# First store of a pairwise product held for a later load piece, and its last three pairs sent in nine transfers of falling height

## The chip, the cores and the metric

The kernel runs on one core of one Trainium2 chip. The metric is device time in microseconds for one execution: the median of several runs, each without the profiler's own account. One further execution was profiled; its trace is what the views below are read from.

## The reference

For 4096 samples with 32 fields of 64 numbers each, every field is multiplied by a 64 x 64 matrix, and then every pair of fields (i < j, 496 pairs) gives the elementwise product of the raw field i and the transformed field j:

```python
vid = jnp.einsum('bfd,de->bfe', x, W)            # x: (4096, 32, 64), W: (64, 64), float32
idx_i, idx_j = jnp.triu_indices(F_, k=1)         # 496 pairs
return x[:, idx_i, :] * vid[:, idx_j, :]         # (4096, 496, 64)
```

The input is 33.6 MB, the output 520 MB, so nearly all the traffic is stores.

## The kernel before, in words

**Layout.** The 128 partitions hold two halves of the batch, 64 embedding numbers each. The free dimension counts in units of `C` = 128 samples, 512 bytes per partition: one unit is one field of a tile, or one pair of the output. The batch makes 16 tiles of 32 fields. Everything lives in one buffer `mem` of 445 units per partition; inputs and output slots are places in it, written out by hand in `XPLACE` (where each tile's fields go) and `SLOTS` (pairs in a slot, its first unit, and where the slot is cut because part of its space comes free earlier). A slot of 96 pairs is thus 128 rows of 49152 bytes, one row per partition.

**Work on one tile.** TensorE makes `vid` (all 32 transformed fields, in PSUM) with eight matmuls (line 172). VectorE then makes the 496 products tile by tile (line 196), in blocks that reuse one field against many, and writes them into the current slot. When the last pair of a slot is done, the slot is stored by one transfer (line 199). There are 70 slots over the 16 tiles; the slots run on across tile borders.

**Order of the work.** The order on SyncE (which issues every transfer) and on VectorE is the program's own. Slots share space: slot 0 (units 221 to 316) is overwritten by slot 2 (200 to 315), so VectorE waits for a store to land before it refills that space. SyncE issues in order, so a transfer that has to wait holds back every later one.

**Loads.** Tile 0 comes in two transfers (lines 136 and 140). The other tiles come in three groups. Right at the start, before the loop, tiles 1 to 3 are loaded in one transfer of 96 fields, and tiles 5 and 4 (64 fields) in two pieces given by `CUTS` (line 153): 38 fields and then 26. Two more groups of five tiles follow later, each in three pieces of which the last is 26 fields.

**The hold.** The first store after each group of loads is made to wait until the last piece but one has landed:

```python
store = nc.sync.dma_start(out=out[:, begin:end, :], in_=ot)
if pieces:
    behind(store, pieces[-2])
    pieces.clear()
```

`behind` adds a dependency: the later instruction is issued when the earlier transfer has landed. For the first store this means: when only the last 26 fields of the load are left.

**Completion semaphores.** Every transfer signals its landing on a semaphore. In the built program the transfers take them in turn from a set of eight (DMAHW0 to DMAHW7), and a transfer whose semaphore was used eight transfers earlier is issued after that one has landed, unless SyncE has waited for it already.

Of the kernel before, what the change touches and what calls it, by code (L numbers as in the profile page):

```python
# [21 lines left out]
    [[6, 7, 8, 9, 10]],  # L22
    [[15, 14, 13, 12, 11]],
]
CUTS = [[None, [(0, 38), (38, 64)]], [(0, 127), (127, 134), (134, 160)], [(33, 160), (26, 33), (0, 26)]]
XPLACE = [317, 349, 381, 413, 32, 0, 285, 317, 349, 381, 413, 128, 96, 64, 32, 0]


# [9 lines left out]
    (126, 247), (127, 96), (109, 223), (112, 333), (127, 158), (127, 285), (127, 64, 94),  # L38
    (127, 192, 93), (124, 320), (120, 48), (127, 190), (124, 317), (125, 158),
]  # L40


PAD = 24
# [9 lines left out]
def by_block():  # L53


    def within(lo):
        yield "step", lo, 2, 1, 0
        for k in range(2):
            yield "step", lo, 4, 2, k
        for i in (lo, lo + 8):  # L60
            yield "row", i + 4, i, 4, 4
        yield "row", lo + 8, lo, 8, 8

    yield from within(0)
    yield "row", 16, 0, 16, 16
    yield from within(16)


def products(blocks, at=0):

    for kind, a, b, c, d in blocks:
        if kind == "row":
            rows, n, i0, di, j0, dj = c, d, b, 0, a, 1
        else:
            rows, n, i0, di, j0, dj = 16 // b, c, a, b, a + c + d, b
        r = k = 0
        while r < rows:
            room = BREAKS[bisect_right(BREAKS, at)] - at
            if k or room < n:
                m, w = 1, min(n - k, room)  # L80
            else:
                m, w = min(rows - r, room // n), n
            yield at, m, w, i0 + r * di + k, di, j0 + r * dj, dj
            at += m * w
            if k + w == n:
                r, k = r + m, 0
            else:
                k += w
# [10 lines left out]
@with_exitstack  # L99
def pairwise_bilinear_kernel(  # L100
    ctx: ExitStack,
    tc: tile.TileContext,
    x0: bass.AP,
    x: bass.AP,
    out: bass.AP,
):

    nc = tc.nc
    NT = sum(len(tiles) for group in GROUPS for tiles in group)
    F = x0.shape[1] - 1 - PAD0
    D = P // 2
    NP = F * (F - 1) // 2

    BANK = 512 // C


    ctx.enter_context(tc.manual_schedule(engines={mybir.EngineType.SP, mybir.EngineType.DVE}))

    const = ctx.enter_context(tc.tile_pool(name="const", bufs=1))
    psum = ctx.enter_context(
        tc.tile_pool(name="ps", bufs=1, space=bass.MemoryType.PSUM)
    )
    vid = psum.tile([P, F, C], F32)

    mem = const.tile([P, UNITS, C], F32)


    w2 = const.tile([P, P], F32)


    place = XPLACE[0]
    nc.sync.dma_start(
        out=mem.rearrange("p u c -> p (u c)")[:, place * C - D : (place + F // 2) * C],
        in_=x0.rearrange("p u c -> p (u c)")[:, C - D : (1 + F // 2) * C],
    )
    nc.sync.dma_start(out=mem[:, place + F // 2 : place + F, :], in_=x0[:, 1 + F // 2 : 1 + F, :])  # L140
    nc.vector.memset(w2, 0.0)  # L141
    for half in (slice(0, D), slice(D, P)):
        nc.vector.tensor_copy(w2[half, half], mem[half, place - 1, C - D :])  # L143
    loaded = 1

    def load(tiles, cuts=()):
        nonlocal loaded
        n = len(tiles) * F
        place = XPLACE[tiles[0]]
        at = (loaded - 1) * F  # L150
        loaded += len(tiles)
        return [
            nc.sync.dma_start(out=mem[:, place + lo : place + hi, :], in_=x[:, at + lo : at + hi, :])  # L153
            for lo, hi in cuts or [(0, n)]
        ]

    ready = mybir.DependencyInfo(mybir.DependencyClass.Sync, mybir.DependencyReason.DATA)

    def behind(later, earlier):
        tc.add_manual_dep(later.ins, earlier.ins.name, ready, reason="issued when that has landed")  # L160

    pieces = []
    groups, cuts = iter(GROUPS), iter(CUTS)
    for tiles, parts in zip(next(groups)[1:], next(cuts)):
        pieces = load(tiles, parts)

    for t in range(NT):
        xt = mem[:, XPLACE[t] : XPLACE[t] + F, :]


        for b in range(0, F, BANK):
            nc.tensor.matmul(  # L172
                vid[:, b : b + BANK, :],
                lhsT=w2,
                rhs=xt[:, b : b + BANK, :],
                start=True,
                stop=True,
            )

        for at, m, w, i, di, j, dj in products(by_block(), t * NP):  # L180
            slot = bisect_right(STARTS, at) - 1
            n = m * w
            begin, end = STARTS[slot], STARTS[slot + 1]
            ot = mem[:, SLOTS[slot][1] : SLOTS[slot][1] + SLOTS[slot][0], :]
            o = ot[:, at - begin : at - begin + n, :]
            if m == 1:
                left = xt[:, i : i + w, :]
                right = vid[:, j : j + 1, :].to_broadcast([P, w, C])
            else:
                o = o.rearrange("p (m w) c -> p m w c", m=m)  # L190
                right = vid[:, j : j + (m - 1) * dj + 1 : dj, :].unsqueeze(2).to_broadcast([P, m, w, C])
                if di == 0:
                    left = xt[:, i : i + w, :].unsqueeze(1).to_broadcast([P, m, w, C])
                else:
                    left = xt.rearrange("p (m d) c -> p m d c", d=di)[:, i // di : i // di + m, i % di : i % di + w, :]
            nc.vector.tensor_tensor(o, left, right, ALU.mult)  # L196
            at += n
            if at == end:
                store = nc.sync.dma_start(out=out[:, begin:end, :], in_=ot)  # L199
                if pieces:  # L200
                    behind(store, pieces[-2])
                    pieces.clear()


        if t + 2 == loaded < NT:
            (tiles,) = next(groups)
            pieces = load(tiles, next(cuts))
# [45 lines left out]
```

## Time and profile before

| | |
|---|---|
| median of 3 runs | 1286.8 us (1286.73 to 1287.43) |
| the profiled execution's own time | 1287.24 us |
| its span, first to last instruction | 1285.5 us |
| VectorE busy | 1084.0 us, 84% |
| TensorE matmul busy | 231.1 us, 18% |
| DMA queue | 553.69 MB, 99.8% of 16 engines' span |
| first store issued; slot 1's; slot 2's | 28.78; 41.95; 61.49 us |

The busy share of an engine is time in instructions over the span. The share of the DMA queue is the time of its packets over 16 engines' span: 100% means that every one of the 16 engines always has a packet in hand. A packet is one row of a transfer (one partition's contiguous bytes), or the small write that signals an engine's part of a transfer as landed. SPq is SyncE's queue: the time shown beside a transfer there is that of issuing it, not of moving its bytes. The columns of a wait are: who waited (engine and line), for whom, us in total, times, longest us.

### The profile page before, as it was taken

Reading aid. Unit: us, or ns where it says so; the run is one execution under the profiler, and the core shown is the slowest. Engines: PE = TensorE matmul, PEld = TensorE weight load, DVE = VectorE, ACT = ScalarE, POOL = GpSimd, SP = SyncE. Lnnn points to the kernel's source line nnn. Section 1 sums busy time; section 2 is a strip of 40 time slices with the busy share of each in tenths; the row PEclk is TensorE's granted clock in tenths of the full one; section 3 lists DMA queues with packets and bytes.
Section 4 is the critical chain, followed back from the end, with each engine's and each line's share of the span. In section 5 each row is a group of like instructions: output and inputs, shape, how many; then the busy total and the mean of one; then the engine's idle time right before and its main releaser. Section 6 shows DMA issues by size and latency. Waiting matters only on the chain.

```text
span 1285.5 us, 1143 instructions
## 1 busy us (share of the span) xinstructions
PE 231.1 (18%) x256; PEld 67.7 (5%) x256; DVE 1084.0 (84%) x348; POOL 0.2 (0%) x4
## 2 busy tenths in 40 slices
PE   5031121303120212040311211103122130312000
PEld 1000000100000000010000000000000010000000
DVE  6889998899967389899799992849998889999952
POOL 0000000000000000000000000000000000000000
PEclk8555565556555556555565555556555555555555
DMA  9999999999999999999999999999999999999998
GB/s 400 438 429 438 436 428 438 431 435 436 432 430 439 416 433 425 445 430 433 439 427 441 435 429 436 419 432 429 440 432 440 429 430 441 429 441 430 434 436 370
DMA packets 11670, 553.75 MB, mean 431 GB/s; under 512 B 1296, under 2 KB 1296, under 8 KB 1552
## 3 DMA queue, kind: packets, MB, share of 16 engines
q1 hardware_dynamic: 11664, 553.69, 99.8%
q8 instruction: 2, 0.03, 0.0%
q14 instruction: 4, 0.03, 0.0%
HBM read 33.59 MB, written 520.09 MB: 431 GB/s over the span
## 4 chain that ended last, share of the span: by engine, by line
DVE 47%; DMA 44%; issue 6%; PE 0%; DVEq 0%; SPq 0%
DVE mem L196 47%; DMA out_dram<-mem 41%; DMA mem<-in_r_x_dram 3%; PE vid L172 0%; DVEq L241 0%; DVEq L196 0%; DVE w L143 0%; SPq L153 0%; DVEq L143 0%; SPq L199 0%
## 5 line engine op out<-in xcount | busy, mean ns | idle before, releaser
L196 DVE TENSOR_TENSOR mem<-mem,vid 128x1024 f32<-128x1024 f32 (+17 forms) x345 | 1083.4, 3212 | 170.5 <-DMA out_dram<-mem 164.2
L172 PE MATMUL vid<-mem,w 128*128 128x512 f32 x256 | 231.1, 1039 | 951.3 <-DVE mem L196 843.8
L172 PEld LDWEIGHTS vid<-mem,w 128*128 128x128 f32 x256 | 67.7, 306 | 1113.5 <-DVE mem L196 1011.9
L143 DVE COPY w<-mem 64x64 f32<-64x64 f32 x2 | 0.4, 190 | 5.0 <-DMA mem<-in_r_x_dram 4.9
L141 DVE MEMSET w<- 128x128 f32 x1 | 0.2, 165 | 0.8 <-PEq L221 0.8
L221 POOL MEMSET const-bfloat16-1.0<- 128x1 bf16 x1 | 0.1, 101 | 0.0
L221 POOL MEMSET const-uint8-127<- 128x1 uint8 x1 | 0.1, 101 | 0.0
L221 POOL MEMSET const-float32-0.0<- 128x1 f32 x1 | 0.1, 98 | 0.2 <-issue 0.2
L221 POOL MEMSET const-float32-1.0<- 128x1 f32 x1 | 0.1, 98 | 0.0
## 6 DMA issues: line engine op xcount, KB each, us to landing
out_dram<-mem SPq DMA_DIRECT2D x15, 8128.0 KB, 27.4
out_dram<-mem SPq DMA_DIRECT2D x14, 7680.0 KB, 24.9
out_dram<-mem SPq DMA_DIRECT2D x6, 7168.0 KB, 26.2
out_dram<-mem SPq DMA_DIRECT2D x5, 7936.0 KB, 28.2
out_dram<-mem SPq DMA_DIRECT2D x3, 7424.0 KB, 22.6
out_dram<-mem SPq DMA_DIRECT2D x3, 5888.0 KB, 20.9
mem<-in_r_x_dram SPq DMA_DIRECT2D x2, 8128.0 KB, 37.6
out_dram<-mem SPq DMA_DIRECT2D x2, 8064.0 KB, 24.3
```

The lines of the kernel that those rows point to most:

```text
L141: nc.vector.memset(w2, 0.0)
L143: nc.vector.tensor_copy(w2[half, half], mem[half, place - 1, C - D :])
L172: nc.tensor.matmul(vid[:, b : b + BANK, :], lhsT=w2, rhs=xt[:, b : b + BANK, :], start=True, stop=True,)
L196: nc.vector.tensor_tensor(o, left, right, ALU.mult)
L221: nc = _bacc.Bacc("TRN2", target_bir_lowering=False, num_devices=1, dynamic_dma_scratch_size=512)
```

## The change

Two things are edited. The cut of the second load piece moves from field 38 to field 51, so that the first store is issued when 13 fields of the load are left instead of 26. And slot 0's store sends only its first 93 pairs as one transfer; its last three pairs (`TAIL`) go out in nine transfers that take the partitions in turn: 64 of them, then 14, 12, 10, 8, 8, 6, 4 and 2 (`ROWS`), with 1536 bytes per partition each. All nine stand behind the 93-pair store and ahead of slot 1's store on SyncE. The dependency of the hold is on the 93-pair store. All other slots are stored as before.

```diff
-CUTS = [[None, [(0, 38), (38, 64)]], [(0, 127), (127, 134), (134, 160)], [(33, 160), (26, 33), (0, 26)]]
+CUTS = [[None, [(0, 51), (51, 64)]], [(0, 127), (127, 134), (134, 160)], [(33, 160), (26, 33), (0, 26)]]
...
+TAIL = 3
+ROWS = [64, 14, 12, 10, 8, 8, 6, 4, 2]
...
             if at == end:
-                store = nc.sync.dma_start(out=out[:, begin:end, :], in_=ot)
+                cut = SLOTS[slot][0] - (TAIL if slot == 0 else 0)
+                store = nc.sync.dma_start(out=out[:, begin : begin + cut, :], in_=ot[:, :cut, :])
+                if begin + cut < end:
+                    for lo, n in zip(accumulate([0, *ROWS]), ROWS):
+                        rows = slice(lo, lo + n)
+                        nc.sync.dma_start(out=out[rows, begin + cut : end, :], in_=ot[rows, cut:, :])
                 if pieces:
                     behind(store, pieces[-2])
                     pieces.clear()
```

## The prediction

> **What bounds the kernel now.** I read the page from its second part down: who is busy in every slice, the queue that carries it, then the first 80 us by engine, and last SyncE's own waits.
>
> ```profile
> span 1285.5 us, 1143 instructions
> ...
> PE 231.1 (18%) x256; PEld 67.7 (5%) x256; DVE 1084.0 (84%) x348; POOL 0.2 (0%) x4
> ...
> DMA  9999999999999999999999999999999999999998
> ...
> q1 hardware_dynamic: 11664, 553.69, 99.8%
> HBM read 33.59 MB, written 520.09 MB: 431 GB/s over the span
> ```
>
> The DMA row is nine in every slice but the last, and the one queue occupies 99.8% of 16 engines' span. VectorE is busy 84%. So the kernel is the time of 553.69 MB through 16 DMA engines, plus whatever idle or slowed time an engine picks up. The end is set by the engine that picked up most.
>
> The trace's packet records give that per engine. A store of 96 pairs is 128 rows of 49152 B, eight on each engine, and an undisturbed row takes 1.815 us; a 13312 B row (26 fields) takes 0.498, a 3584 B row 0.140. Following each engine's rows from transfer to transfer:
>
> ```
> end of transfer, us             first    mean     last engine
> load piece of 38 fields          27.51    27.88    28.30
> load piece of 26 fields          31.53    32.42    33.57
> store of slot 0                  46.03    46.91    48.07
> store before the second load    404.83   405.32   405.57
> last store                     1281.39  1282.04  1284.28
> ```
>
> Subtracting undisturbed row times leaves lateness. It grows where loads turn into stores: mean and worst engine go from 2.62 and 3.05 us to 3.20 and 4.35 at 33 us, from 4.15 and 4.55 to 4.65 and 6.45 at 430 us, and from 5.47 and 6.49 to 5.77 and 7.91 at 833 us. It ends at 6.12 and 8.35. Ahead of the second and third loads the early engines are slowed towards the latest one (mean 3.52 to 4.07 at 404 us, worst unchanged at 4.33). So **what counts is how late the last engine is**; an early engine's lead is not kept.
>
> SyncE around the first hold, from its waits between 28 and 64 us and its timeline to 70 us:
>
> ```profile
> SPq L199 <- DVE mem L196: 32.3, 3, 19.2
> SPq L199 <- DMA mem<-in_r_x_dram: 25.3, 1, 25.3
> ```
>
> ```profile
> 0.73 0.37 SPq L136 DMA_DIRECT2D mem<-in_r_x_dram  x1
> 1.16 0.42 SPq L140 DMA_DIRECT2D mem<-in_r_x_dram  x1
> 1.63 1.80 SPq L153 DMA_DIRECT2D mem<-in_r_x_dram  x3
> 28.78 33.04 SPq L199 DMA_DIRECT2D out_dram<-mem  x3
> ```
>
> The first store waits 25.3 us for the 38-field piece and then 0.3 for VectorE, and goes out at 28.78. The three stores of the last line begin at 28.78, 41.95 and 61.49: slot 1 is issued four us before the first engine finishes slot 0 (46.03), so no engine runs dry.
>
> [...] rows follow each other without a gap at the 46 us change. [...] this trace shows 1.0 (issue at 0.73, first row at 1.735)[...].
>
> **The change part by part.**
>
> *The hold.* 51 fields land instead of 38. A 26112 B row costs 0.724 + 6656 x 36.8 ps = 0.969 us (36.8 ps per byte is 1.675 us over 45568 B, from the rows above), eight rows take 1.96 us more, so the piece ends at 30.25 on the last engine instead of 28.30. VectorE finished at 28.78 and no longer matters; the store goes out at about 30.4, 1.65 us later. In before, rows of the last piece begin to stretch at 29.98, which is 1.2 us after the issue (0.498 grows to as much as 1.2 us), and cost 0.58 us in the mean and 1.30 on the worst engine. After: 30.4 + 1.2 = 31.6, when undisturbed loads end between 31.5 and 32.3. Most of that stretch goes: the last engine would end the loads at 32.3 to 32.8 instead of 33.57, **a gain of 0.8 to 1.3 us there**. It may instead leave a gap of up to 0.5 us on the first engines, whose lead counts for nothing. Nothing else is issued in that time on SyncE.
>
> *The split.* Slot 0's store becomes 93 pairs (rows of 47616 B, 1.759 us) and nine transfers of 1536 B rows, each an estimated 0.140 - 2048 x 36.8 ps = 0.065 us. [...] Against eight rows shortened by 0.056 (0.45 us) and 9 ns per completion packet that is +0.4 us on the lowest engines and -0.2 on the highest. Bytes are unchanged. VectorE and TensorE instructions are the same.
>
> *The wait that comes with it.* This decides. In the built program every transfer takes the next of eight completion semaphores, and an issue waits until the transfer eight before it has landed. Before: slot 0 is the sixth transfer, so slot 1 and the next stores wait for loads long done. After: the order on SyncE is 93 pairs (sixth), 64, 14, 12, 10, 8, 8, 6, **4, 2**, then slot 1. The four-partition transfer takes the 93-pair store's semaphore and **waits for that store to land**; the two-partition one waits for the 64-partition one. Slot 1, all its VectorE work done at 41.95, stands behind both. The rings hold only 0.3 to 0.7 us of small rows after the 93 pairs.
>
> Working it out: loads end at 31.5 to 32.8; eight rows of 1.759 take 14.05; the 93 pairs end at 45.6 on the first engine and about 46.8 on the last. Landing to SyncE is 0.35 us (in before 48.07 to 48.42), so the four-partition issue goes at 47.1, the next at 47.5, slot 1 at 47.9 (issues follow each other by 0.43 to 0.47 in the lines above). Idle restart is not shown in mid-kernel. From below it is 1.0 us, the first packet after the first issue; from above the cold start's full lateness, 1.9 us in the mean and 2.3 on the worst engine after issue. A store reads SBUF and not HBM, so I take 1.5 in the mean and 2.0 on the last: slot 1 begins at 49.4 in the mean, 49.9 at the last, against 46.91 and 48.07. **Loss: 2.5 us in the mean, 1.8 on the last engine** (1.0 to 2.2 for the bounds). The hold's gain and the skewed rows are already inside this; after the restart the engines are aligned again, so the skew is spent.
>
> Who else waits: VectorE's refill of slot 0's space waits for the 93 pairs (47.1 instead of 48.42, a gain in cover) and its last four pairs for all nine small transfers (down by about 50); it is then in an 11.4 us chain of products, so that wait is hidden. Later stores are issued 2.7 us or more ahead of the rings (61.49 against 64.15) and shift with the landings they follow, so nothing further runs dry.
>
> *Later.* At 404 us the others are pulled to the last engine; an aligned pack has no lone straggler, so each gets a part of the stretch, +0.1 to +0.4 on the last. The next two turns I leave as they were, +1.9 and +1.4 on the worst, with an uncertainty of about 1 us together. Sum: +1.8 + 0.1 = +1.9 us. Against the profiled execution's own 1287.24 (span 1285.5 and 1.74 around it) that is 1289.1; that run lies 0.4 over the median, so on the median 1286.8 it is **1288.7**.
>
> **Rivals.** (1) *The restart costs its upper bound and the aligned pack pays more at the next load*: slower. Place: slot 1's first rows, and 404 us. Price: 2.2 + 0.4 + one turn worse by 0.5 = +3.1, 1289.9. It decides once slot 1's last engine begins after about 50.6 (48.07 + 2.57). For it: cold-start rows took up to 1.39 us instead of 0.32. Against: those were HBM reads. (2) *Alignment pays*: two engines alone end 1.6 us behind the other 14 (1283.77 and 1284.27 against 1282.65 and less), having taken 1.45 each at 833 us; if an aligned pack has no such pair, 1.5 comes off, and with a restart at the lower bound the total is -0.5, 1286.3. Against: the spread before each turn was only 0.8 to 1.7 us already and still opened to 2.0 to 3.1. (3) *The wait doesn't empty the rings*, because the small rows[...] take several times 0.065, or the issue waits less than it seems: only hold and skew remain, about -1, 1285.8. Against: slot 0's 14 us must still land first.
>
> **How the numbers follow.** A measurement of this kernel can tell about 0.2%, 2.57 us. Forecast 0.55, rival 1 0.27, rival 2 0.13, rival 3 0.05. Rival 1 is mostly beyond the bound and the forecast's upper tail adds a little: slower 0.32. Rivals 2 and 3 lie mostly within: faster 0.03. The range takes in rival 2 and rival 1's price: 1286.3 to 1290.4.
>
> **What would show it.** Right: SyncE waits some 13 us on a store from about 34 us and issues slot 1 near 48 instead of 41.95; the GB/s row dips between 46 and 50 us; first store issued near 30.4. Wrong: slot 1's rows begin before 48, or all engines restart later than 50.6; or the last engine's lag behind the mean at the end differs from 2.2 us by more than 1.

## Result and the profile after

The changed kernel takes 1289.68 us (median of 14 runs, 1288.96 to 1290.15) against 1286.84 for the kernel before in the same runs (14 runs, 1285.79 to 1287.53): +2.84 us, a ratio of 1.0022 (95% interval 1.0014 to 1.003). The interval, 1.8 to 3.9 us, excludes zero: the change makes the kernel slower, by close to the 2.57 us that the prediction took as the least that can be told, and the time lies inside its range. The profiled execution of the changed kernel is the fastest of its runs (1288.96), that of before lies 0.4 over its median, so the two traces differ by only 1.7 us; where the trace accounts for less than the medians, that is why.

The lines of the changed kernel's page that answer to those of before: the queue is as full as it was, to a tenth of a percent.

```profile
span 1287.2 us, 1160 instructions
...
PE 227.0 (18%) x256; PEld 66.1 (5%) x256; DVE 1084.0 (84%) x348; POOL 0.2 (0%) x4
...
DMA  9999999999999999999999999999999999999998
...
q1 hardware_dynamic: 11872, 553.69, 99.7%
HBM read 33.59 MB, written 520.09 MB: 430 GB/s over the span
```

The average hides the place. SyncE's waits between 28 and 64 us in the changed kernel (line, for whom: us in total, times, longest), and then its timeline (start, us, what):

```profile
SPq L204 <- DMA mem<-in_r_x_dram: 27.3, 1, 27.3
SPq L204 <- DVE mem L200: 11.9, 1, 11.9
SPq L208 <- DMA out_dram<-mem: 7.4, 1, 7.4
```

```profile
30.73 0.35 SPq L204 DMA_DIRECT2D out_dram<-mem  x1
31.12 16.20 SPq L208 DMA_DIRECT2D out_dram<-mem  x9
47.42 12.75 SPq L204 DMA_DIRECT2D out_dram<-mem  x2
```

The third wait is the one that the change adds: one of the nine transfers (line 208) waits 7.4 us for a store. The trace names the semaphores. The 93-pair store is the first transfer to signal on number 106, and its last engine does so at 46.75; the four-partition transfer, eight later, waits for 106 and is issued at 46.76. The two-partition one waits for 107, the 64-partition transfer's, and is issued at 47.06. Slot 1 goes out behind both, at 47.42 instead of 41.95. It shows in the rings, the rows that each engine has in hand. Columns of the next two lines: window, its length, busy time of PE, PEld, DVE and POOL, TensorE clock, share of the DMA engines, GB/s. First the kernel before, then the changed one:

```profile
45.00:50.00 5.00, 0.00 (x0) 0.00 (x0) 1.48 (x1) 0.00 (x0) 0.50 0.98 423
```

```profile
45.00:50.00 5.00, 0.00 (x0) 0.00 (x0) 3.34 (x3) 0.00 (x0) 0.50 0.61 236
```

In the mean an engine is without a packet for 1.6 of these five microseconds (packet records, clipped to the window; the view counts a packet where it starts), and for 1.0 us all 16 are; in the kernel before no engine runs dry. The same records by engine: the 93-pair store ends between 45.72 and 46.34, the last of the first seven small transfers at 46.97, the 4- and 2-partition ones run alone from 47.51 to 47.93, and slot 1 begins on all 16 engines between 48.27 and 48.42.

The chain of waits of the changed kernel from 28 to 64 us says it too; after the loads it goes from the store to SyncE and back to a store, where that of before went to VectorE. First the kernel before, then the changed one:

```profile
28.78 19.64 DMA out_dram<-mem
...
50.05 11.42 DVE mem L196 x2
...
61.49 22.57 DMA out_dram<-mem
```

```profile
2.11 28.54 DMA mem<-in_r_x_dram
...
30.73 16.02 DMA out_dram<-mem
...
46.76 0.25 SPq L208
...
47.06 1.20 DMA out_dram<-mem
```

### The profile page after: what moved, and what is told of

Read it like the earlier page. It is cut to its first block, busy times and chain, and to the rows that moved or that the text cites. A ratio compares the mean times of both kernels' runs of the same rounds, so it can differ in the third digit from the quotient of the medians.

```text
span 1287.2 us, 1160 instructions
## 1 busy us (share of the span) xinstructions
PE 227.0 (18%) x256; PEld 66.1 (5%) x256; DVE 1084.0 (84%) x348; POOL 0.2 (0%) x4
## 3 DMA queue, kind: packets, MB, share of 16 engines
q1 hardware_dynamic: 11872, 553.69, 99.7%
## 4 chain that ended last, share of the span: by engine, by line
DMA 46%; DVE 44%; issue 7%; DVEq 0%; SPq 0%
DVE mem L200 44%; DMA out_dram<-mem 41%; DMA mem<-in_r_x_dram 5%; DVEq L250 0%; SPq L157 0%; DVEq L200 0%; SPq L144 0%; SPq L140 0%; SPq L208 0%; SPq L204 0%
## 5 line engine op out<-in xcount | busy, mean ns | idle before, releaser
L176 PE MATMUL vid<-mem,w 128*128 128x512 f32 x256 | 227.0, 1021 | 957.5 <-DVE mem L200 849.2
```

The source lines that it names most:

```text
L176: nc.tensor.matmul(vid[:, b : b + BANK, :], lhsT=w2, rhs=xt[:, b : b + BANK, :], start=True, stop=True,)
```

## The experiments

All times are medians; the difference is to the kernel before measured beside it. Single runs of one kernel lie up to 0.5 to 1 us from its median, and the intervals are about 1 us to either side, so that differences of a few tenths between rows of this table are not clear of noise by themselves. "Long rows" are rows of 32 pairs (16384 B) instead of three (1536 B).

```
kernel                               us        difference   ratio, 95% interval
late hold alone                      1287.30      +0.46     1.0006  0.9997 to 1.0014
late hold, slot 1 waits for slot 0   1288.91      +2.07     1.0017  1.0010 to 1.0024
late hold, six transfers, no wait    1287.90      +1.06     1.0009  1.0001 to 1.0017
late hold, eight even transfers      1288.94      +2.10     1.0017  1.0010 to 1.0024
late hold, nine nearly even          1289.47      +2.72     1.0021  1.0012 to 1.0029
nine transfers, early hold           1290.58      +3.83     1.0029  1.0018 to 1.0040
first hold at 40 fields              1286.65      -0.10     1.0000  0.9991 to 1.0008
all three holds at 13                1287.51      +0.76     1.0005  0.9997 to 1.0013
third hold at 13                     1287.68      +0.73     1.0006  0.9997 to 1.0014
six long-row transfers, no wait      1296.09      +9.14     1.0070  1.0058 to 1.0083
wait, then six long-row transfers    1298.68     +11.73     1.0089  1.0076 to 1.0103
one long-row transfer, 128 high      1287.38      +0.09     1.0001  0.9992 to 1.0010
```

The second table follows the engines through the profiled executions, from the packet records: by how much a stage ends later than in the kernel before, in the mean of the 16 engines / on the last engine, us (read to about 0.03). Every row is one execution against one execution of the kernel before.

```
                       first loads    slot 1        before load 2   at load 2      last store
                       (33 us)        (66 us)       (387 us)        (405 us)       (1284 us)
changed kernel         -0.57/-1.27    +1.53/+0.45   +2.18/+1.66     +2.46/+2.41    +2.81/+1.63
late hold alone        -0.64/-1.43    -0.61/-1.43   -0.11/-0.58     +0.16/+0.17    +0.15/+0.43
hold, slot 1 waits     -0.64/-1.41    +1.27/+0.20   +1.92/+1.40     +2.24/+2.19    +2.41/+1.61
six transfers          -0.66/-1.46    -0.25/-0.98   +0.12/-0.24     +0.46/+0.61    +0.45/+0.45
nine, early hold       +0.20/-0.21    +2.53/+1.44   +3.28/+4.14     +3.55/+4.14    +4.12/+2.96
first hold at 40       +0.66/+0.15    +0.67/+0.15   +0.40/+0.15     -0.07/+0.15    -0.41/-1.02
all holds at 13        -0.62/-1.34    -0.52/-1.34   +0.01/-0.49     +0.24/+0.31    +1.42/+0.24
```

### The late hold alone

```diff
-CUTS = [[None, [(0, 38), (38, 64)]], ...
+CUTS = [[None, [(0, 51), (51, 64)]], ...
```

> Only the cut moves (51 and 13 fields); slot 0 is stored whole, as before, and no store waits for another. Theory (the wait on slot 0's landing is the loss, the later hold a small gain): loads end near 31.6 to 32.3 us as in the changed kernel, slot 1 is issued at about 42, slot 0 ends by 46.8 on the last engine and slot 1's rows follow without a gap; the time is 0.3 to 1.0 us under the kernel before. Rival (the later hold is itself the loss, by starving engines or by lining them up before the second load): 1 us or more above the kernel before.

The first half came as expected: the loads end 1.43 us earlier on the last engine, slot 1 goes out at 41.10. The time did not: +0.46, an interval that includes zero. The table shows where it went. The gain is whole at 66 us, 0.5 of the mean is gone by 387, and at 405 nothing is left. On the last engine it goes in two steps: 0.74 us within one store at 151 us, when a short packet of the instruction queue falls on one engine (more on this below), and 0.75 us at the second load, where the engines are levelled. It is not a loss of its own either.

### The wait without the nine transfers

On top of the late hold:

```diff
+                if slot == 0:
+                    first = store
+                if slot == 1:
+                    behind(store, first)
```

> The cut moves, slot 0 is stored whole, and slot 1's store is made to wait until slot 0's store has landed: the wait without any of the nine transfers. Theory: it shows nearly the whole loss of the changed kernel. Slot 0 ends by 46.8 us on the last engine, landing at 47.2, slot 1 issued at 47.2, first rows near 48.1 on all engines within 0.2 us; 2.0 to 3.0 us above the kernel before. Rival (the small transfers with their issue time of over 1 us each, or their rows of unlike number, are the loss): within 0.7 us of the kernel before.

+2.07, as the theory had it. SyncE's waits in this kernel between 28 and 50 us:

```profile
SPq L199 <- DMA mem<-in_r_x_dram: 27.3, 1, 27.3
SPq L199 <- DMA out_dram<-mem: 16.1, 1, 16.1
```

One wait, on the same landing, gives 1.6 us over the late hold alone and about three quarters of the changed kernel's loss, without a single small transfer.

### Six transfers that leave no wait

```diff
-ROWS = [64, 14, 12, 10, 8, 8, 6, 4, 2]
+ROWS = [64, 16, 16, 14, 10, 8]
```

> The cut moves and slot 0's last three pairs go out in six transfers of 64, 16, 16, 14, 10 and 8 partitions. Slot 1's store then takes the semaphore of the last load piece, landed long before, and waits for no store. Theory: the rings never empty, slot 1's rows follow the small rows on each engine; 0 to 1 us under the kernel before. Rival (small transfers cost): 1.5 to 3 us above it.

Slot 1 goes out at 42.24 and its rows follow the small ones without a gap: the window from 45 to 50 us is as full as in the kernel before.

```profile
45.00:50.00 5.00, 0.00 (x0) 0.00 (x0) 3.51 (x3) 0.00 (x0) 0.50 1.07 433
```

So the wait is gone, and with it 1.8 of the 2.8 us. But +1.06 lies above the 0 to 1 us *under* that I expected: 0.6 over the late hold alone. Slot 1 ends 0.36 later in the mean than there; the 1536 B rows took 98 ns in the mean and up to 445 instead of 65. So small transfers cost something, well below the rival's figure of 1.5 to 3.

### Eight even transfers, and nine nearly even ones

```diff
+ROWS = [16, 16, 16, 16, 16, 16, 16, 16]
```

> The cut moves and slot 0's last three pairs go out in eight transfers of 16 partitions, one row on every engine each, so that every engine has eight small rows. The eighth takes the 93-pair store's semaphore and waits for it, slot 1 stands behind it. Theory: rows of unlike number count for nothing, since the wait lines the engines up anyway; one issue fewer behind the wait, so 0 to 0.3 us less than the changed kernel, 2.3 to 3.0 us above the kernel before. Rival (the unlike rows make the loss): within 1 us of the kernel before.

```diff
+ROWS = [16, 16, 16, 16, 16, 16, 16, 8, 8]
```

> As the changed kernel, but the nine transfers take 16 partitions seven times and 8 twice, so that an engine has nine or seven small rows and not 12 to 4; two transfers wait, as in the changed kernel. If the second issue behind the wait is what sets the changed kernel 0.7 us over the one with eight even transfers: slot 1 issued near 47.4 and 2.4 to 3.0 us above the kernel before. Rival (the unlike rows): 1.8 to 2.3 above it.

With eight, +2.10: the rows of unlike number are not the loss, and the result equals that of the wait alone. With nine, +2.72, beside the changed kernel's +2.84: the slope of the rows, an estimated 12 to 4 on an engine, makes no difference that can be told. The ninth transfer puts a second issue behind the wait. Slot 1 goes out at 47.12 with eight and 47.47 with nine, which is 0.35 of the 0.6 us between them; for the rest I have no place, and the two intervals overlap.

### The nine transfers with the early hold

```diff
-CUTS = [[None, [(0, 51), (51, 64)]], ...
+CUTS = [[None, [(0, 38), (38, 64)]], ...
```

> The nine transfers as in the changed kernel, but the first store held as before, for 38 fields. Theory (with the wait in place the last engine's end of slot 0 decides when slot 1 restarts, so here the later hold does help): loads end at about 33.5 us on the last engine, the 93 pairs at 47.6, slot 1 issued near 48.7 and begun near 49.6, some 1.2 us later than in the changed kernel; 3.3 to 4.5 us above the kernel before. Rival (the later hold is a loss of its own in the changed kernel): 1.5 to 2.5 us above the kernel before.

+3.83, within what was expected. Waits of this kernel between 28 and 50 us:

```profile
SPq L204 <- DMA mem<-in_r_x_dram: 25.3, 1, 25.3
SPq L208 <- DMA out_dram<-mem: 10.4, 1, 10.4
```

Slot 1 is issued at 48.42, one microsecond later than in the changed kernel, since the last engine ends the loads later. So the late hold, worth nothing by itself, is worth 1.0 us where a wait on the last engine follows before the next load; slot 1 ends 1.0 us earlier for it in the mean and on the last engine. (The +4.14 at 387 us in the table has a reason of its own: in that execution a packet of the instruction queue, 0.92 us at 331.7, falls on one engine; the changed kernel's comes at 432.6.) The two halves of the change are not independent.

### The hold moved the other way

```diff
+CUTS = [[None, [(0, 24), (24, 64)]], ...
```

> No split; the first store is released earlier, with 40 fields of the load left (cut at 24) instead of 26. VectorE ends slot 0 at 28.8 us, so the store goes out at 28.8 at the earliest, as before, whatever the load does. Theory: the loads end as in the kernel before or up to 0.3 us later and the time is within 0.4 us of the kernel before. Rival (the piece's size itself matters, not the time of release): 0.5 us or more from the kernel before in either direction.

The time is that of before (-0.10) though the loads end 0.66 us later in the mean. At 405 us the mean is within 0.07. With the late hold this brackets it: ends of the first loads that differ by 1.3 us in the mean are within 0.23 at the second load. One line of my expectation was wrong: the store went out at 26.55, so VectorE's slot 0 was done by then, and not only at 28.78.

### Later holds elsewhere

```diff
+CUTS = [[None, [(0, 51), (51, 64)]], [(0, 127), (127, 147), (147, 160)], [(33, 160), (13, 33), (0, 13)]]
```

> No split; all three holds release when 13 fields are left, so the second and third groups too. Theory (a stretch at a turn from loads to stores that comes ahead of another load is levelled out there, one that comes last is kept): lateness grows by under 0.2 us in the mean at 430 and 833 us instead of 0.50 and 0.30; only the last of the two reaches the end, so 0.2 to 1.0 us under the kernel with the first hold alone, about level with the kernel before or up to 0.6 below. Rival (each turn's gain is kept): 1.5 us or more below the kernel before.

```diff
+CUTS = [[None, [(0, 38), (38, 64)]], [(0, 127), (127, 134), (134, 160)], [(33, 160), (13, 33), (0, 13)]]
```

> No split, first and second hold as before; only the third group's hold releases at 13 fields left. Theory: up to 827 us as the kernel before; the loads end at about 0.3 us less in the mean and 1.2 to 1.5 us less on the last engine; then the aligned engines creep by some 0.8 us to the end, so the time is between 0.6 us under and 0.5 us above the kernel before. Rival (the gain of the last turn is kept whole): 1.0 us or more below it.

Both missed, +0.76 and +0.73, and differently; neither rival came true either. With all three late the turns are gentle as expected: the last engine's lateness at 833 us is 1.15 below that of before, the spread 0.65 instead of 3.07 us. Then the mean, relative to before, rises from +0.56 at 833 us to +1.42 at the end. With the third alone late, the engines come to that turn spread by 2.5 us. SyncE's waits between 820 and 850 us:

```profile
SPq L199 <- DMA mem<-in_r_x_dram: 38.4, 1, 38.4
SPq L199 <- DVE mem L196: 0.9, 1, 0.9
```

The piece lands with its last engine at 832.09, the store goes out at 832.55, and 15 engines begin it between 833.39 and 833.54 though many had ended their loads a microsecond or more before: the rings ran empty and the mean jumps by 1.39 us. Thirteen fields, 2.0 us of rows, don't cover a spread of 2.5.

### Spreading the engines on purpose

```diff
-TAIL = 3
+TAIL = 32
+ROWS = [64, 16, 16, 14, 10, 8]
```

> The cut moves; slot 0's last 32 pairs (16384 B rows, 0.611 us each) go out in six transfers of 64, 16, 16, 14, 10 and 8 partitions, so that engines 0 to 7 have nine such rows, 8 and 9 eight, 10 to 13 seven, 14 and 15 six; no store waits for another. This spreads the engines by up to 1.8 us on purpose. Theory (engines that run within a fraction of a microsecond of each other slow each other, and the second load levels the rest): the spread after slot 0 is 1.5 to 2.5 us against 0.6 with the late hold alone; from 66 to 387 us the mean lateness creeps by 0.2 to 0.5 us instead of 0.5 to 0.7; at 404 us all is levelled and the time is within 0.7 us of the kernel before. Rival (the creep is not a matter of alignment): it creeps by 0.6 us or more.

The same rows, cut off slot 1 in the kernel where slot 1 waits for slot 0:

```diff
-                cut = SLOTS[slot][0] - (TAIL if slot == 0 else 0)
+                cut = SLOTS[slot][0] - (TAIL if slot == 1 else 0)
...
+                if slot == 0:
+                    first = store
+                if slot == 1:
+                    behind(store, first)
```

> The cut moves, slot 0 is stored whole, slot 1 waits for its landing, and slot 1's last 32 pairs go out in six transfers of 64, 16, 16, 14, 10 and 8 partitions: the wait lines the engines up, the rows spread them again by 1.8 us. Theory: slot 1's whole rows still show the slowing of aligned engines (61440 B rows at 2.279 us had 2.267 in the kernel before), later slots do not (59392 B rows back from 2.199 to about 2.192), the mean creeps by 0.2 to 0.5 us from 84 to 387 us instead of 0.6, and the time is within 0.6 us of the kernel with the wait alone, since the last engine is the later one by the spread. Rival: 59392 B rows stay at 2.198 us or more, with the same creep.

Both failed as experiments on alignment: they are 9 and 12 us slower for a reason of their own. The 16384 B rows, expected at 0.611 us, took 1.27 in the median and up to 6.7 in the first of the two (1.27 and 6.8 in the second), and its first engine began slot 1 at 47.8, the last at 54.8. The queue of the first has 11872 packets, 208 more than before: 128 rows of these and 80 completions, and 80 is 16 + 16 + 16 + 14 + 10 + 8. The 64-partition transfer comes first on every engine: once all 16 are in it, its rows take 1.27 us one like the other, twice 0.611. The rows of several microseconds come after it, in the transfers of 16 partitions and fewer. The page of the first of the two shows it in its second slice:

```profile
GB/s 407 346 428 432 437 432 433 434 437 428 431 446 406 426 436 430 441 423 445 427 439 426 433 440 438 419 425 430 445 430 439 439 424 434 423 443 427 434 438 385
```

To see whether it was the size of the rows or the height of the transfers (their number of partitions):

```diff
-ROWS = [64, 16, 16, 14, 10, 8]
+ROWS = [128]
```

> As the kernel with six staggered transfers of 32 pairs (9 us slower than before), but these 32 pairs go out in one transfer of all 128 partitions: the same 16384 B rows, eight on every engine. Theory (it is the small number of partitions that slows those rows, 1.27 us in the median and up to 6.7, not their size or being split off): rows of 0.611 us with a mean under 0.63, slot 1's rows following without a gap, and the time of the kernel with the late hold alone, 0 to 1.0 us above the kernel before. Rival (rows split off are slow at any height): rows of 1 us or more and 5 us or more above it.

The same rows in one transfer of 128 partitions: 0.611 in the median, 0.613 in the mean, 0.636 at most, and +0.09 us. So neither their size nor their being split off slows them; it is the small height.

## Why the prediction was right or wrong

**The mechanism was right.** The four-partition transfer waits for the 93-pair store, slot 1 stands behind it, the rings run empty. The issue times were 46.76, 47.06 and 47.42 against 47.1, 47.5 and 47.9 predicted; the 93 pairs ended at 45.72 to 46.34 against 45.6 to 46.8. The wait alone reproduces about three quarters of the loss, and removing it removes 1.8 of the 2.8 us. The number of engines of a small transfer, which before with its 128 partitions everywhere could not show, is in the changed kernel's trace: the nine signal 16, 14, 12, 10, 8, 8, 6, 4 and 2 landings, where a transfer of 128 partitions signals 16: one for each engine that took part. The queue has 208 packets more (11872 against 11664), 128 small rows and 80 completions, the sum of these. From 12 small rows on some engines down to 4 on others, and the skew of +0.4 and -0.2 us that goes with it, is an estimate from these counts: it takes the smaller transfers to run on engines that the larger ones use too.

**The sum came out 0.9 us low, and that it came so near is in part luck: terms that were off by more than that had opposite signs.**

- *The restart was oversized.* I took 1.5 us from issue to rows in the mean and 2.0 on the last engine, an estimate between two bounds from the loads at the start, nearer the cold start's lateness; nothing in before showed a restart of stores. Measured: 0.85 to 1.00 us, on all 16 engines within 0.15, with first rows of 2.30 to 2.31 us instead of 2.27. The lower bound was the right one. Slot 1 begins 1.4 us later than before in the mean and 0.35 on the last engine, not 2.5 and 1.8. (The bounds themselves were added up wrongly: 1.0 and 2.3 us after 47.9 give 0.8 and 2.1 on the last engine, not 1.0 and 2.2.)
- *What an aligned pack costs later was undersized.* I wrote +0.1 us on the last engine; it goes from +0.45 at 66 us to +2.41 at 405. Two steps make most of that. At 134.7 us a packet of the instruction queue (0.31 us) falls on one engine, between two rows, and stretches those two by 0.27 and 0.36 us. Within one store that engine is 0.84 us behind the mean, where the last engine was 0.10 behind; by 387 us the mean has come up to 0.29 behind it. The kernel before has the same packet at 151.2 us, on an engine that is not the last, and there the last engine's lag does not grow (1.12 and then 1.05 us). The late hold alone, the wait alone and the eight even transfers show the jump too (0.19 to 0.83, 0.10 to 0.84, 0.11 to 0.84). The other step is the second load: 0.75 us on the last engine, 0.3 in the mean. An engine's lead was, against what I wrote, a reserve: a pack without early engines has none that can be delayed for nothing.
- *The two later turns were left as they were.* In the traces the last engine gains there on that of before, from +2.41 at 405 us to +1.63 at the end. With this the traced executions differ by less than the 1.9 us of the sum, not by more; that the medians differ by 2.84 is therefore not placed engine by engine.

One of the prediction's own signs of being wrong did come: the last engine's lag behind the mean at the end, 2.24 us before, was to stay within 1 us of 2.2 and is 1.05. It concerns the terms after the restart, not the wait.

**The hold.** The step "most of that stretch goes" held (1.27 us off the last engine, 0.8 to 1.3 predicted). That its gain was "already inside" the restart was right for the changed kernel, as the early-hold experiment shows by its 1.0 us. For the hold alone the rival's "about -1" failed: the levelling at the second load, which the prediction itself described, takes about half of the gain, and the instruction packet the other half.

**A misreading.** I took the 0.3 us beside VectorE in SyncE's waits, and its product ending at 28.78, as the end of slot 0. The experiment with 40 fields issued the store at 26.55. That product belonged to slot 1; the store had waited for the landing alone, which took 0.48 us from last row to issue in both kernels (28.30 to 28.78, 30.25 to 30.73). The predicted issue at 30.4 was 0.3 early for that reason.

**Small rows.** The estimate of 0.065 us is the median measured; the mean is 0.085, the longest 0.287. Their issue was mis-sized: seven took 0.55 to 1.42 us on SyncE instead of 0.43 between starts, so that SyncE's wait was 7.4 us from 39.3 and not some 13 from 34. That was hidden, since the next issue had to wait until 46.7 anyway.

**The rivals.** Rival 1 had the side on which the result fell, and its 1289.9 lies nearer than the forecast: its second half (an aligned pack pays more at the next load) happened, with 0.75 us where it had 0.4, its first (a restart at the upper bound, last engine after 50.6) did not; slot 1 began at 48.42. Rival 2 is refuted in its total: alignment did not pay. In the traced execution the last engine does lie only 1.05 us behind the mean instead of 2.24, as that rival hoped, but the mean itself had moved by 2.81. Rival 3, no wait, is refuted by the trace; its time of -1 is also wrong, since the six transfers without a wait are 1.06 over.

**Open.** Why the rows of engines in step take a few nanoseconds longer, and why the engines are levelled ahead of a load, was not isolated, because the experiments meant for it were spoiled by the short transfers. Nor is the last 0.3 us between eight and nine transfers placed. None of the variants beats the kernel before by more than the noise.

## What to carry to other kernels

Count completion semaphores before cutting a transfer up: six extra pieces cost 0.6 us here, but with eight semaphores the eighth transfer after the big one waits for it to land (7.4 us in the changed kernel), and everything behind it in the queue waits too (slot 1, issued at 47.42 us instead of 41.95). When a queue is full for 99.8% of the time, follow each engine's lateness from stage to stage: a gain ahead of a point where the engines are levelled was lost there (late hold alone: 0.58 us on the last engine at 387 us, nothing at 405), while a gap that moved all of them was kept (wait alone: +1.27 us in the mean at 66 us, +2.41 at the end). Where all engines run in step, a short delay can make the one that it hits the last (a packet of 0.31 us at 134.7 us in the changed kernel). A held store needs cover: here the rows left would have had to outlast the spread of the engines plus the 1.3 us from the last row through issue to the first row of the store (832.09 to 833.39 with the third hold late).

## What the runs showed of the hardware that I had not expected

- **Transfers of few partitions can be far slower per row.** 16384 B rows took 1.27 us in a transfer of 64 partitions and up to 6.7 us in those of 16 to 8; in a transfer of 128 partitions 0.613 in the mean. Why was not shown: no run here isolates it. The 1536 B rows are not slowed in the median, which in the changed kernel is 0.065 us, the undisturbed estimate.
- **Engines in step run slightly slower.** With all 16 within 0.15 us, 61440 B rows of slot 1 took 2.279 us in the mean (changed kernel, wait alone, eight even), or 2.275 without the first row after the restart, against 2.267 where they were spread by 2.03 and 0.69 us (before, six transfers) and 2.269 at 0.55 (late hold alone). The mean of the changed kernel loses 0.65 us against before from 66 to 387 us, an estimate of 4 ns for each of the 152 rows that an engine stores in that time.
- **A restart of stores is quick:** in the changed kernel 0.85 us from the start of the issue to the first row, 0.15 us between engines, against 1.0 us and 0.64 at the cold start. Counted from the end of the issuing instruction the two are 0.49 and 0.63 us.
- **An instruction packet on one engine can decide who is last.** In before, one engine stands still for 1.12 us at 430 us, beside a packet of the instruction queue of 1.14 us at 429.8; in the changed kernel a packet of 0.31 us at 134.7 stretches two rows of one engine by 0.27 and 0.36 us and makes it the last of the aligned pack.
